# Moving a query's weights into retired memory and the first query ahead of the token loop

## The chip, the cores and the metric

The kernel runs on one core of a Trainium2 chip. The metric is the device time of one execution in microseconds (us). The times shown are the median of three runs. A profile records one execution more; its span, from the first to the last instruction, is a little shorter than the time of the execution it was taken from. Engines are named as in the profile: PE is TensorE (its weight loads, PEld, overlap its products), DVE is VectorE, ACT is ScalarE, POOL is GpSimd, SP is SyncE, whose queue issues nearly all plain transfers here.

## The reference

One graph block over 1250 nodes of 768 features, with 41,250 edges: a graph attention network of two layers and a linear attention side by side, and then a mixture of experts.

```python
xn = layernorm(x)
# graph: 4 heads of 192, then 2 heads of 96, softmax over each node's incoming edges
out2 = gat(gat(norm(xn), W1, 4 heads), W2, 2 heads)
gnn = concat([xn, out2]) @ Wu + bu
# linear attention, 12 heads of 64, phi(t) = elu(t) + 1
q, k, v = phi(xn @ Wq + bq), phi(xn @ Wk + bk), xn @ Wv + bv
kv, ksum = sum_n k[n] v[n]^T, sum_n k[n]            # by head
mix = ((q @ kv) / (q . ksum)) @ Wo + bo
x = x + gnn + mix
# experts: 8, the best two of a gate for each node, hidden width 384
y = layernorm(x)
x = x + sum_e gate_e(y) * (gelu(y @ W1[e] + b1[e]) @ W2[e] + b2[e])
```

## The kernel before, in words

All of it is one function, `gps_block`. Nodes are worked on in NT = 10 tiles of PT = 125, features in KC = 6 slices of 128, and a product of one tile with a 768 x 768 weight is 2 halves of 384 columns with 6 slices each, thus 12 products. They are in float32, and each is two records in the profile.

The stages follow each other in the source: edges are turned into a dense count matrix `AT` and node features are normalised and turned into `xnT` (L358 to L369); first-layer features of all nodes go to `gw`, a view of the tile `kept` (L426 to L436); the first graph attention runs over 4 heads (L542 to L558), the second over 2 (L564 to L574), whose result `o2T` is also a view of `kept`. Then come keys and values (L598 to L629): for each node tile 12 products with `Wk_sb`, 12 with `Wv_sb` and 6 that add k v^T to `kvacc`. L637 to L647 add the values' bias, mask the blocks of the heads, and turn `kvacc` into `kvT` and `ksum` by TensorE transposes (L644, L645) and ScalarE copies (L646, L647). L679 to L684 multiply `kvT` into `Wo_sb`, so that one product with the query gives the linear attention's output. L671 to L677 fold the biases bo and b2 into `bu_b`.

Then the loop over ten node tiles (L767 to L854): `query(t)` (L741 to L764) is 12 products with `Wq_sb` (L750), a chain of steps on VectorE with one exponential on ScalarE (L752 to L761), and six transposes into `qT` (`turn`, L319, L321). `query(t + 1)` is called ahead of tile t's output: 12 products on `xnT` with `Wu_sb` and 12 on `qT` with `Wo_sb` (L780), 4 on `o2T` with `Wu2_sb` (L791), additions on VectorE (L782, L785, L793), a layer norm, the gate and the ranking of the experts. The first query stands ahead of the loop (L766). Last come the experts, with weights in a ring of four buffers of the pool `wt` (L653 to L662, L690, L858, L948 to L957).

What sets the order: a framework that builds the program orders the instructions of each engine itself. Each engine then works through its own list, and instructions wait on semaphores. So a step can stand earlier in an engine's list than in the source: keys' and values' products run in TensorE's gaps of the two attentions, from 132.9 us on. It also places pools in on-chip memory, as stacks from the left and from the right side, and a tile whose place overlaps an earlier one waits until that was last used. Before the change the pool `wt` with Wo, Wq, Wu and Wu2 (L584 to L593) lies where the graph's tiles (`AT`, `mask`, `h2`) were, which are given back at L581 when the second attention is over. The small row tiles bq, bu, bo and bv lie in `kept`, and their loads stand in SP's queue ahead of the weights'.

Of the kernel before, what the change touches and what calls it, by code (L numbers as in the profile page):

```python
# [27 lines left out]
F32 = mybir.dt.float32  # L28
# [5 lines left out]
AF = mybir.ActivationFunctionType  # L34
ALU = mybir.AluOpType
AX = mybir.AxisListType
PSUM = bass.MemoryType.PSUM

N, D = 1250, 768
PT, NT = 125, 10  # L40
KC = D // 128
H1, C1, H2, C2 = 4, 192, 2, 96
HEADS, DH = 12, 64
# [17 lines left out]
def row_bcast(ap, parts):  # L61

    n = 1
    for s in ap.shape:
        n *= s
    return bass.AP(tensor=ap.tensor, offset=ap.offset, ap=[[0, parts], [1, n]])
# [3 lines left out]
def gps_block(ctx: ExitStack, tc: tile.TileContext, x, src, dst, norm_g, norm_b, W1, a_src1, a_dst1,  # L70
# [11 lines left out]
    const = ctx.enter_context(tc.tile_pool(name="const", bufs=1))  # L82
    small = ctx.enter_context(tc.tile_pool(name="small", bufs=3))
    dram = ctx.enter_context(tc.tile_pool(name="dram", bufs=1, space=bass.MemoryType.DRAM))
    big = ctx.enter_context(tc.tile_pool(name="big", bufs=1))
    xr = x.rearrange("(t p) d -> p t d", p=PT)

    def token_rows(t):
# [7 lines left out]

    o0 = H2 * N
    o2T = kept[:C2 + 1, :o0].rearrange("p (h n) -> p h n", h=H2)
    kvT = kept[:, o0:o0 + D].rearrange("p (c f) -> p c f", c=KC)
    ksum, bq_b, bu_b, bo_b = (kept[:PT, o0 + k * D:o0 + (k + 1) * D] for k in range(1, 5))  # L100
    setup = ExitStack()
    fl = setup.enter_context(tc.tile_pool(name="fl", bufs=1, side="right"))
    blocks128 = [(r0, min(T, r0 + 128)) for r0 in range(0, T, 128)]
# [24 lines left out]
    def bank(pool=None, name="mm"):  # L128
        return (pool or mm_p).tile([128, 512], F32, name=name)
# [196 lines left out]
    with tc.tile_pool(name="ma_p", bufs=2, space=PSUM) as ma_p:  # L326
# [111 lines left out]
        with tc.tile_pool(name="hot", bufs=2) as hot, \  # L438
                tc.tile_pool(name="ec_p", bufs=2, space=PSUM) as ec_p:
            for t in range(NT):  # L440
                for i in range(t * NC // NT, (t + 1) * NC // NT):
                    chunk(i, hot, ec_p)
                features(t)
                if t == 1:
                    weights()
                    setup.close()
                    kp = kps.enter_context(tc.tile_pool(name="kp", bufs=1, side="right"))
                    Wk_sb = kp.tile([128, KC, D], F32)
                    Wv_sb = kp.tile([128, KC, D], F32)
                    bk_b = kp.tile([PT, D], F32)  # L450
                    kvacc = kp.tile([128, KC, 129], F32)
                if t == 4:
                    nc.sync.dma_start(Wk_sb, Wk.rearrange("(c p) f -> p c f", p=128))
                    nc.sync.dma_start(Wv_sb, Wv.rearrange("(c p) f -> p c f", p=128))
                    nc.sync.dma_start(bk_b, row_bcast(bk, PT))
# [84 lines left out]
    with tc.tile_pool(name="wp", bufs=3) as wp, tc.tile_pool(name="rb", bufs=1) as rb:  # L540
        with tc.tile_pool(name="ag_p1", bufs=1, space=PSUM) as ag_p:
            for hd in range(H1):  # L542
                ag = ag_p.tile([PT, NT // 2, 512], F32, name="ag")

                def gather1(st, w):
                    for t in range(NT):
                        o = (t % 2) * CG
                        nc.tensor.matmul(ag[:, t // 2, o:o + CG], w[:, t * PT:(t + 1) * PT],  # L548
                                         gw[:, st, hd], start=st == 0 and t % 2 == 0,
                                         stop=st == NT - 1, skip_group_check=True)  # L550

                attend(s1[:, :, hd, 0], s1[:, :, hd, 1], lo1[:, :, hd], wp, rb, gather1)
                v = ag[:, :, :2 * CG].rearrange("p a (b c) -> p a b c", b=2)
                rd = small.tile([PT, NT // 2, 2, 1], F32, name="rd")
                nc.vector.reciprocal(rd, v[:, :, :, C2:C2 + 1])
                for t in range(NT):
                    nc.vector.scalar_tensor_tensor(h2[:, t], v[:, t // 2, t % 2], rd[:, t // 2, t % 2],
                                                   h2[:, t], op0=ALU.mult, op1=ALU.add)  # L558
        ones2 = h2[:, :, :2 * (C2 + 1)].rearrange("p t (h c) -> p t h c", h=H2)[:, :, :, C2:]
        nc.vector.memset(ones2, 1.0)  # L560
        at = 2 * (C2 + 1)
# [19 lines left out]
    graph.close()  # L581


    wt = ctx.enter_context(tc.tile_pool(name="wt", bufs=1))  # L584

    def weight(w):
        t = wt.tile([128, KC, D], F32, name="w", bufs=4)
        nc.sync.dma_start(t, w.rearrange("(c p) f -> p c f", p=128))
        return t

    Wo_sb, Wq_sb, Wu_sb = weight(Wo), weight(Wq), weight(Wu[:D])
    Wu2_sb = wt.tile([96, H2, D], F32)
    nc.sync.dma_start(Wu2_sb, Wu[D:].rearrange("(c p) f -> p c f", p=96))  # L593
    for t, a in ((bq_b, bq), (bu_b, bu), (bo_b, bo)):
        nc.sync.dma_start(t, row_bcast(a, PT))


    for t in range(NT):  # L598
        ky = kp.tile([PT, D], F32, name="ky", bufs=2)
        va = kp.tile([PT, KC, 129], F32, name="va")  # L600
        nc.gpsimd.memset(va[:, :, 128:], 1.0)
        for k in range(2):
# [25 lines left out]
            else:  # L628
                nc.vector.tensor_copy(acc, got)  # L629

    pair = kp.tile([128, 128], F32)
    nc.gpsimd.memset(pair, 0.0)
    nc.gpsimd.memset(pair[0:DH, 0:DH], 1.0)
    nc.gpsimd.memset(pair[DH:128, DH:128], 1.0)
    bv_b = kept[:, o0 + 5 * D:o0 + 6 * D]
    nc.sync.dma_start(bv_b, row_bcast(bv, 128))
    for c in range(KC):  # L637
        acc = kvacc[:, c, :128]
        kcol = kvacc[:, c, 128:]
        nc.vector.scalar_tensor_tensor(acc, bv_b[:, c * 128:(c + 1) * 128], kcol, acc, op0=ALU.mult,  # L640
                                       op1=ALU.add)
        nc.vector.tensor_mul(acc, acc, pair)
        ps = bank()
        nc.tensor.transpose(ps[:, :128], acc, ident)  # L644
        nc.tensor.transpose(ps[:PT, 128:256], kcol.to_broadcast([128, PT]), ident)  # L645
        nc.scalar.copy(kvT[:, c], ps[:, :128])  # L646
        nc.scalar.copy(ksum[:, c * 128:(c + 1) * 128], ps[:PT, 128:256])  # L647
    kps.close()


    fp = ctx.enter_context(tc.tile_pool(name="fp", bufs=1, side="right"))
# [15 lines left out]
    nc.sync.dma_start(Wg_sb, Wg.rearrange("(c p) e -> p c e", p=128))  # L667
    bg_b = fp.tile([PT, NE], F32)
    nc.sync.dma_start(bg_b, row_bcast(bg, PT))
    nc.gpsimd.tensor_add(bu_b, bu_b, bo_b)  # L670
    for k in range(2):  # L671
        half = slice(k * 384, (k + 1) * 384)
        ps = bank()
        for h in range(H2):
            nc.tensor.matmul(ps[:PT, :384], col96[:, 8 + h:9 + h].to_broadcast([96, PT]),
                             Wu2_sb[:, h, half], start=h == 0, stop=h == H2 - 1)
        nc.vector.tensor_add(bu_b[:, half], bu_b[:, half], ps[:PT, :384])  # L677

    for c in range(KC):  # L679
        for k in range(2):  # L680
# [6 lines left out]
    nc.gpsimd.memset(zero, 0.0)  # L687
    nc.sync.dma_start(xl_d[N:], zero)
    nc.sync.dma_start(out[N:], zero[:, :D])
    ring = [expert(fW1[0], fW2[0], fb2[0])]  # L690
    outr = out[:N].rearrange("(t p) d -> p t d", p=PT)
    xlr = xl_d[:N].rearrange("(t p) d -> p t d", p=PT)
    idx = fp.tile([128, NV + 1], I32)
# [4 lines left out]
    with ExitStack() as rs:  # L698
# [7 lines left out]
        def numbers(shape, pattern, base, mult, name, dt=F32):  # L706
# [2 lines left out]
                           allow_small_or_imprecise_dtypes=True)  # L709
            return t  # L710

        before = numbers([PT, NE, NE], [[1, NE], [-1, NE]], 0, 0, "before")
        nc.vector.tensor_scalar(before, before, 0.0, None, op0=ALU.is_gt)
        upto = numbers([128, NE, NE], [[1, NE], [-1, NE]], 0, 0, "upto")
# [23 lines left out]
        cum = rp.tile([PT, NT + 1, NE], F16)  # L738
        nc.vector.memset(cum[:, 0], 0.0)
        inv = g_p.tile([128, NV], F32, name="inv", bufs=1)  # L740
        def query(t):  # L741
            tk = slice(t * PT, (t + 1) * PT)

            qy = qp.tile([PT, D], F32, name="qy")
            qe = qp.tile([PT, D], F32, name="qe", bufs=1)
            for k in range(2):
                half = slice(k * 384, (k + 1) * 384)
                ps = bank()
                for c in range(KC):
                    nc.tensor.matmul(ps[:PT, :384], xnT[:, c, tk], Wq_sb[:, c, half], start=c == 0,  # L750
                                     stop=c == KC - 1)
                nc.vector.tensor_add(qy[:, half], ps[:PT, :384], bq_b[:, half])  # L752
            nc.vector.tensor_scalar(qe, qy, 0.0, None, op0=ALU.min)
            nc.scalar.activation(qe, qe, AF.Exp)
            nc.vector.scalar_tensor_tensor(qy, qy, 0.0, qe, op0=ALU.max, op1=ALU.add)
            nc.vector.tensor_mul(qe, qy, ksum)
            den = rl.tile([PT, HEADS, 1], F32, name="den")
            nc.vector.tensor_reduce(den, qe.rearrange("p (h d) -> p h d", h=HEADS), AX.X, ALU.add)
            nc.vector.reciprocal(den, den)
            q_h = qy.rearrange("p (h d) -> p h d", h=HEADS)  # L760
            nc.vector.tensor_mul(q_h, q_h, den.to_broadcast([PT, HEADS, DH]))  # L761
            qT = qp.tile([128, KC, PT], F32, name="qT")
            turn(qT, qy, mm_p, "mm", nc.scalar.copy)
            return qT  # L764

        qT_next = query(0)  # L766
        for t in range(NT):  # L767
            tk = slice(t * PT, (t + 1) * PT)
            xt = qp.tile([PT, D], F32, name="xt")
# [85 lines left out]
        free = rp.tile([128, NV], F32)  # L855
        nc.vector.tensor_scalar(free, inv, 0.0, nobody, op0=ALU.is_equal, op1=ALU.mult)
        nc.vector.scalar_tensor_tensor(idx[:, :NV], inv, -1.0, free, op0=ALU.add, op1=ALU.add)
        for e in range(1, 4):  # L858
            ring.append(expert(fW1[e], fW2[e], fb2[e]))


# [30 lines left out]


    mix.close()
    sp = ctx.enter_context(tc.tile_pool(name="sp", bufs=2))
    x_p = ctx.enter_context(tc.tile_pool(name="x_p", bufs=1, space=PSUM))
    h_p = ctx.enter_context(tc.tile_pool(name="h_p", bufs=2, space=PSUM))
# [117 lines left out]
```

## Time and profile before

| what | us |
|---|---|
| median of 3 runs | 1166.87 (1166.84 to 1167.5) |
| the profiled execution | 1167.08 |
| its span | 1165.0 |
| edges, features, first-layer weights, to | 196 |
| first graph attention, to | 460 |
| second graph attention, to | 591 |
| rest of keys and values, to | 607.85 |
| first work with Wu, Wu2 and Wo, to | 617.47 |
| loop over node tiles, to | 909 |
| routing and first gather, to | 937 |
| experts, to | 1165 |

The limits of the stages are read from the timeline; the first ones overlap a little. Over the span PE is busy 1066.3 us (92%), DVE 665.0 (57%), ACT 358.1 (31%), POOL 76.5 (7%); the mean granted TensorE clock is 0.975 of full speed. A row of the page gives the busy time of a group of instructions, the mean of one in ns, and the idle time of its engine just before them with what ended it.

### The profile page before, as it was taken

What the parts mean: (1) busy time and instruction counts of PE and PEld (TensorE: products, weight loads), DVE (VectorE), ACT (ScalarE), POOL (GpSimd) and SP (SyncE); (2) the same over time, 40 slices, a digit from 0 to 9 for tenths busy, and PEclk for the clock granted to TensorE, in tenths of its full rate; (3) what the DMA queues carried; (4) which work ended last, traced back from release to release, by engine and by line L of the source; (5) the groups of instructions that cost most, each with busy time, mean ns of one, the idle gap of its engine ahead of it and who ended that gap; (6) DMA issues with size and microseconds to landing.
All of it is one profiled execution on the core that took longest, in us unless ns stands there. A gap on an engine that the chain in (4) does not pass through costs nothing.

```text
span 1165.0 us, 12068 instructions
## 1 busy us (share of the span) xinstructions
PE 1066.3 (92%) x4542; PEld 712.8 (61%) x4542; DVE 665.0 (57%) x1359; ACT 358.1 (31%) x527; POOL 76.5 (7%) x99
## 2 busy tenths in 40 slices
PE   2699998999999989988989999999999599999994
PEld 2596655578787869544545666666666356666652
DVE  7866676669696967688842455555555422222211
ACT  2141114373737364283822211111111011211111
POOL 1000000000000000000000000000000122322321
PEclk9999999999999999989999999999999789999997
DMA  5014000000000001000064011111113637777633
GB/s 158 27 49 168 14 27 1 1 1 1 1 1 1 1 1 54 1 0 1 1 262 165 27 41 41 40 40 41 43 44 117 227 84 189 212 209 217 123 55 56
DMA packets 34823, 79.76 MB, mean 68 GB/s; under 512 B 6799, under 2 KB 14561, under 8 KB 34749
## 3 DMA queue, kind: packets, MB, share of 16 engines
q1 hardware_dynamic: 29148, 59.06, 15.4%
q0 software_dynamic: 5600, 19.77, 8.4%
q8 instruction: 39, 0.64, 0.2%
q14 instruction: 36, 0.29, 0.1%
HBM read 60.48 MB, written 18.34 MB: 68 GB/s over the span
## 4 chain that ended last, share of the span: by engine, by line
PE 70%; DVE 20%; DMA 3%; issue 2%; ACT 2%; POOL 0%; DVEq 0%; SPq 0%; POOLq 0%; ACTq 0%
PE po L780 14%; PE ph L925 9%; PE py L937 7%; PE mm L430 7%; PE mm L607 7%; PE mm L750 7%; DVE scr L515 6%; DVE w L535 5%; DVE w L536 5%; PE ag L548 3%; PE ag L569 2%; PE u L791 2%; PE mm L405 2%; PE px L909 2%; DMA w<-in_L_gnn_Wu_dram 2%
## 5 line engine op out<-in xcount | busy, mean ns | idle before, releaser
L548 PE MATMUL ag<-kept,w 125*125 125x198 f32 x800 | 137.4, 333 | 5.1 <-DVE w L536 4.9
L548 PEld LDWEIGHTS ag<-kept,w 125*125 125x125 f32 x800 | 133.5, 188 | 9.0 <-DVE w L536 9.0
L925 PE MATMUL ph<-xsT,w 128*128 128x384 f32 (+1 forms) x324 | 100.3, 469 | 1.7 <-DVE xsT L912 1.7
L937 PE MATMUL py<-w,hT 128*128 128x384 f32 x300 | 100.6, 486 | 0.0
L430 PE MATMUL mm<-Wg,xnT 128*125 128x400 f32 x240 | 90.2, 513 | 1.1 <-DVE xnT L321 0.6
L607 PE MATMUL mm<-Wv_sb,xnT 128*125 128x384 f32 x240 | 85.7, 489 | 4.8 <-DVE kvacc L627 4.8
L535 DVE TENSOR_TENSOR w<-v,w 125x1250 f32<-125x1250 f32 x60 | 86.4, 1455 | 6.6 <-ACT w L533 5.9
L515 DVE CUSTOM_DVE_ANT_0 scr<-ss_row,mask 125x1250 bf16<-125x1250 f32 x60 | 87.3, 1455 | 0.5 <-ACT ss_row L506 0.2
L780 PE MATMUL po<-w,xnT 128*125 128x384 f32 x240 | 84.5, 501 | 2.9 <-DMA w<-in_L_gnn_Wu_dram 2.9
L536 DVE SCALAR_TENSOR_TENSOR w<-w,AT 125x1250 f32<-125x1250 f32 x60 | 86.5, 1456 | 0.4
L925 PEld LDWEIGHTS ph<-xsT,w 128*128 128x128 f32 x324 | 59.6, 193 | 41.1 <-DVE xsT L912 2.4
L534 ACT ACTIVATE v<-dn_row,sl 125x1250 f32<-125x1250 f32 x60 | 79.3, 1333 | 16.9 <-DVE w L535 16.4
L607 PE MATMUL mm<-Wk_sb,xnT 128*125 128x384 f32 x240 | 84.4, 486 | 0.0
L750 PE MATMUL mm<-w,xnT 128*125 128x384 f32 x240 | 84.2, 489 | 0.0
L780 PE MATMUL po<-w,qT 128*125 128x384 f32 x240 | 80.8, 487 | 0.0
L937 PEld LDWEIGHTS py<-w,hT 128*128 128x128 f32 x300 | 55.3, 190 | 33.9
L912 DVE COPY xsT<-px 128x384 f32<-128x384 f32 x50 | 25.5, 552 | 85.6 <-PE px L909 46.4
L940 DVE TENSOR_TENSOR ys<-py,wb 128x768 f32<-128x768 f32 x25 | 24.0, 958 | 71.3 <-PE py L937 46.2
L780 PEld LDWEIGHTS po<-w,xnT 128*125 128x125 f32 x240 | 43.3, 190 | 31.2 <-DMA w<-in_L_gnn_Wu_dram 3.1
L780 PEld LDWEIGHTS po<-w,qT 128*125 128x125 f32 x240 | 44.1, 188 | 29.5 <-issue 0.2
L607 PEld LDWEIGHTS mm<-Wv_sb,xnT 128*125 128x125 f32 x240 | 42.4, 187 | 31.1 <-DVE kvacc L627 7.0
L750 PEld LDWEIGHTS mm<-w,xnT 128*125 128x125 f32 x240 | 43.6, 188 | 27.6 <-ACT qT L321 0.2
(269 smaller groups left out, 1388.7 us busy)
## 6 DMA issues: line engine op xcount, KB each, us to landing
w<-in_L_ffn_W_dram SPq DMA_DIRECT2D x18, 1152.0 KB
xt<-in_x_dram SPq DMA_DIRECT2D x20, 336.0 KB
wb<-in_L_ffn_b_dram SPq DMA_DIRECT2D x9, 384.0 KB
out_dram<-xt SPq DMA_DIRECT2D x10, 336.0 KB
xl_d<-xl SPq DMA_DIRECT2D x10, 336.0 KB
W_sb<-in_L_gnn_W_dram SPq DMA_DIRECT2D x1, 2304.0 KB
Wk_sb<-in_L_mix_Wk_dram SPq DMA_DIRECT2D x1, 2304.0 KB
Wv_sb<-in_L_mix_Wv_dram SPq DMA_DIRECT2D x1, 2304.0 KB
```

The costliest lines, as they stand in the source:

```text
L430: nc.tensor.matmul(ps[:PT, :2 * (CG + 2)], xnT[:, c, t * PT:(t + 1) * PT], Wg1[:, c, 2 * k:2 * k + 2].rearrange("p h c -> p (h c)"), start ...
L515: nc.vector.tensor_tensor_reduce(scr, ss_row, mask[:, t], 1.0, 0.0, ALU.mult, ALU.max, top[:, t:t + 1])
L534: nc.scalar.activation(v, dn_row, AF.Exp, bias=sl[:, st:st + 1])
L535: nc.vector.tensor_tensor(w, v, w, op=ALU.max)
L536: nc.vector.scalar_tensor_tensor(w, w, 2.0, AT[:, st, :N], op0=ALU.min, op1=ALU.mult)
L548: nc.tensor.matmul(ag[:, t // 2, o:o + CG], w[:, t * PT:(t + 1) * PT], gw[:, st, hd], start=st == 0 and t % 2 == 0, stop=st == NT - 1, ski ...
L607: nc.tensor.matmul(ps[:PT, :384], xnT[:, c, t * PT:(t + 1) * PT], w[:, c, half], start=c == 0, stop=c == KC - 1)
L750: nc.tensor.matmul(ps[:PT, :384], xnT[:, c, tk], Wq_sb[:, c, half], start=c == 0, stop=c == KC - 1)
L780: nc.tensor.matmul(po[k][:, :384], l, r[:, k * 384:(k + 1) * 384], start=i == 0, stop=i == len(parts) - 1)
L912: nc.vector.tensor_copy(xT[:, 3 * a:3 * a + 3, j * 128:(j + 1) * 128], px[:, a, :384].rearrange("p (b n) -> p b n", b=3))
L925: nc.tensor.matmul(ph[:, :n * 128], w[0][:, o:o + 128], xT[:, c, :n * 128], start=c == 0, stop=c == KC - 1)
L937: nc.tensor.matmul(py[:, k, :384], hT[:, f, j * 128:(j + 1) * 128], w[:, o:o + 384], start=f == 0, stop=f == FC - 1)
```

## The change

Four things move, and the computation stays the same. Wq gets a place in `kept`, where the first layer's gathered features are no longer needed after its last head, and its load stands right behind that layer. The pool `kp` of keys and values now closes before a new pool `mp` (ksum, bq, bu and the queries' tiles) and the pool `wt` (Wo, Wu, Wu2, and the experts' ring) open, all three on the right side. `query` is defined ahead of the product of kvT and Wo, and query 0 is called there. The output's bias is folded on VectorE inside the loop's scope, with bo in an `xt` buffer; bv takes a `ky` buffer. The ring starts with two experts instead of one, and the pool `big` with `xnT` is given back before the experts.

```diff
-    big = ctx.enter_context(tc.tile_pool(name="big", bufs=1))
+    first_half = ctx.enter_context(ExitStack())
+    big = first_half.enter_context(tc.tile_pool(name="big", bufs=1))
...
-    kvT = kept[:, o0:o0 + D].rearrange("p (c f) -> p c f", c=KC)
-    ksum, bq_b, bu_b, bo_b = (kept[:PT, o0 + k * D:o0 + (k + 1) * D] for k in range(1, 5))
+    Wq_sb = kept[:, o0:o0 + KC * D].rearrange("p (c f) -> p c f", c=KC)
+    kvT = kept[:, o0 + KC * D:o0 + KC * D + D].rearrange("p (c f) -> p c f", c=KC)
...
+                    kv = ctx.enter_context(tc.tile_pool(name="kv", bufs=1, side="right"))
+                    kvacc = kv.tile([128, KC, 129], F32)
+                    pair = kv.tile([128, 128], F32)
...
+        nc.sync.dma_start(Wq_sb, Wq.rearrange("(c p) f -> p c f", p=128))
         ones2 = h2[:, :, :2 * (C2 + 1)].rearrange("p t (h c) -> p t h c", h=H2)[:, :, :, C2:]
...
-    wt = ctx.enter_context(tc.tile_pool(name="wt", bufs=1))
...
-    Wo_sb, Wq_sb, Wu_sb = weight(Wo), weight(Wq), weight(Wu[:D])
-    Wu2_sb = wt.tile([96, H2, D], F32)
-    nc.sync.dma_start(Wu2_sb, Wu[D:].rearrange("(c p) f -> p c f", p=96))
-    for t, a in ((bq_b, bq), (bu_b, bu), (bo_b, bo)):
-        nc.sync.dma_start(t, row_bcast(a, PT))
...
-    bv_b = kept[:, o0 + 5 * D:o0 + 6 * D]
+    bv_b = kp.tile([128, D], F32, name="ky", bufs=2)
     nc.sync.dma_start(bv_b, row_bcast(bv, 128))
...
+    kps.close()
+
+    mp = ctx.enter_context(tc.tile_pool(name="mp", bufs=1, side="right"))
+    ksum = mp.tile([PT, D], F32)
+    bq_b = mp.tile([PT, D], F32)
+    bu_b = mp.tile([PT, D], F32)
+    wt = ctx.enter_context(tc.tile_pool(name="wt", bufs=1, side="right"))
...
+    nc.sync.dma_start(bq_b, row_bcast(bq, PT))
+    Wo_sb, Wu_sb = weight(Wo), weight(Wu[:D])
+    Wu2_sb = wt.tile([96, H2, D], F32)
+    nc.sync.dma_start(Wu2_sb, Wu[D:].rearrange("(c p) f -> p c f", p=96))
+    for c in range(KC):
         ps = bank()
-        nc.tensor.transpose(ps[:, :128], acc, ident)
+        nc.tensor.transpose(ps[:, :128], kvacc[:, c, :128], ident)
...
-    nc.gpsimd.tensor_add(bu_b, bu_b, bo_b)
-    for k in range(2):
...
+    def query(t):
...
+        qT = mp.tile([128, KC, PT], F32, name="qT", bufs=2)
+        turn(qT, qy, mm_p, "mm", nc.scalar.copy)
+        return qT
+
+    qT_next = query(0)
 
     for c in range(KC):
         for k in range(2):
...
-    ring = [expert(fW1[0], fW2[0], fb2[0])]
+    ring = [expert(fW1[e], fW2[e], fb2[e]) for e in range(2)]
...
+        bo_b = qp.tile([PT, D], F32, name="xt")
+        for t, a in ((bu_b, bu), (bo_b, bo)):
+            nc.sync.dma_start(t, row_bcast(a, PT))
+        nc.vector.tensor_add(bu_b, bu_b, bo_b)
+        for k in range(2):
+            half = slice(k * 384, (k + 1) * 384)
+            ps = bank(u_p, "u")
+            for h in range(H2):
+                nc.tensor.matmul(ps[:PT, :384], col96[:, 8 + h:9 + h].to_broadcast([96, PT]),
+                                 Wu2_sb[:, h, half], start=h == 0, stop=h == H2 - 1)
+            nc.vector.tensor_add(bu_b[:, half], bu_b[:, half], ps[:PT, :384])
...
-        for e in range(1, 4):
+        for e in range(2, 4):
             ring.append(expert(fW1[e], fW2[e], fb2[e]))
...
     mix.close()
+    first_half.close()
```

## The prediction

> **What bounds the kernel now.** First the chain of waits on the page: TensorE holds 70% of it, so where TensorE stands still the time is lost. Then the same chain between 585 and 662 us, in order of time (start, us, what), because there the moved loads stand:
>
> ```profile
> 591.94 18.81 DMA w<-in_L_gnn_Wu_dram
> 610.75 0.04 issue
> 610.79 2.92 PE po L780 x4
> 613.72 3.92 PE mm L675 x8
> ```
>
> A reader of the chain alone would expect 18.81 us from taking this load off it. The timeline of TensorE (start, us, line, idle before and its releaser) says otherwise: it works off keys and values (L607, L621, L644, L645) until 607.85 and waits only then.
>
> ```profile
> 607.58 0.27 PE L645 MATMUL mm<-ident,kvacc 128*125 128x128 f32 x1
> 610.79 2.92 PE L780 MATMUL po<-w,xnT 128*125 128x384 f32 x4 [2.94 <-DMA w<-in_L_gnn_Wu_dram]
> 613.51 4.12 PE L675 MATMUL mm<-Wu_sb,col 96*125 96x384 f32 x8
> ```
>
> The table by stage (window; length and busy us of PE, PEld, DVE, ACT, POOL; granted clock; DMA share; GB/s) shows what the wait leaves behind:
>
> ```profile
> 607.85:610.79 2.94, 0.00 (x1) 0.00 (x0) 0.53 (x4) 0.43 (x2) 2.74 (x15) 0.77 1.04 386
> 610.79:617.47 6.68, 6.68 (x13) 3.64 (x13) 0.63 (x2) 0.00 (x0) 0.13 (x1) 0.59 1.07 355
> 617.47:660.00 42.53, 42.53 (x137) 23.20 (x136) 14.55 (x21) 10.28 (x22) 0.00 (x0) 1.00 0.19 62
> 718.75:747.50 28.75, 28.75 (x110) 17.56 (x109) 15.23 (x41) 5.39 (x8) 0.00 (x0) 1.00 0.14 41
> ```
>
> The clock is 0.59 for 6.68 us, which costs 0.41 x 6.68 = 2.74. So the weights' wait is worth **2.94 + 2.74 = 5.68 us**. From 617.47 to 909 TensorE has no gap (the loop's window 718.75 to 747.5 is busy for its whole length), so whatever is lost or won before the loop reaches the end undiminished.
>
> **What the change does to the order.** I compared the order in which the two built programs hand instructions to each engine (line numbers here and below are those of before). Up to the end of the second attention TensorE, VectorE and ScalarE have the same order. The title's "beside attention" does not come true: the first query's products stand behind the last transposes of keys and values. After them TensorE has, in order: query 0 (12 products), the transposes of query 0, the 12 products of L683, the bias products of L675, query 1, the 12 products of L780 on xnT, the transposes of query 1, the 12 on qT. Before, L780, L675, L683, L750 and half of L780 stood between the wait and the first transposes. Each of these products is two records in the profile, so 12 are 24 records.
>
> **What goes.** The wait for the weights. Wq is loaded at about 460, when the last L548 has read `kept`, with 130 us to spare. Wo, Wu and Wu2 start later than before, not earlier. SP's queue is worked off in order; in it fb comes first, which waits for the end of attention (590.9), and bq stands ahead of the three, which lies where keys' and values' tiles were and waits for the last L607 and L621 and for the last L640 (606.40 + 0.35). With 0.4 of delay (below) bq goes out at about 607.2. In the trace traffic begins 1.9 us after the first issue (590.92; 592.8 by a table in steps of 2 us, which shows 415 to 418 GB/s), and the last of three weights ends 0.9 us after 7.08 MB at 415 GB/s would (17.06 us, to 609.9; used at 610.79). So Wo (0.38 + 2.36 MB, 6.6 us) is there at 616.6, Wu at 622.3, Wu2 at 623.7. They are wanted at 624, 645 and 635: hidden, by query 0, its chain, and the product. −5.68.
>
> **What comes.** (1) Tail of keys and values. The three transposes of L735 (0.15 each at 618 to 628) move in here, the first behind L580 (594.57 + 0.28), so L621 starts 0.4 later; and ScalarE's copies L646/L647 come in an order that frees each bank one copy (0.27) later. Query 0 starts at 608.6 instead of 607.85: 0.75, of which 0.45 moved: +0.3. (2) Query 0's 24 records at 0.323 (7.75 from 643.45 to 651.20) only move. (3) **The new wait.** The transposes need the whole chain of query 0, and nothing stands between. In the trace:
>
> ```profile
> 635.80 0.56 DVE L752 TENSOR_TENSOR qy<-mm,kept 125x384 f32<-125x384 f32 x1 [2.45 <-PE mm L750]
> 636.98 0.84 ACT L754 ACTIVATE qe<-qe 125x768 f32<-125x768 f32 x1 [8.31 <-DVE qe L753]
> 641.10 0.96 DVE L761 TENSOR_TENSOR qy<-qy,den 125x768 f32<-125x768 f32 x1
> 642.11 0.63 PEld L319 LDWEIGHTS mm<-ident,qy 125*128 125x128 f32 x6 [0.52 <-DVE qy L761]
> ```
>
> From the last product (635.76) to the first transpose 6.35 us; before, L780 and L791 filled them (5.8 + 0.65). Now TensorE stands from 616.35 to 622.7, and L683 queues behind the transposes: +6.35. (4) Clock after that gap: below, +2.0. (5) Query 1's chain now has two L782 additions (0.95 each) in it, so 6.35 + 1.9 = 8.3 against 12 products of L780 (7.75): +0.6.
>
> **Hidden, and what it would cost.** bu + bo leave GpSimd (1.81 at 458, idle there) for VectorE (0.95), behind the load of bu, the last of eight transfers after bq: 10.8 MB at 415 GB/s, so at about 636; wanted at 641, behind query 1's first half (+1 per us once it comes after 643). bq is used at 612.4 and lands at about 611. GpSimd's constants (608.05 to 610.92) move up to 590.8; four short VectorE steps that need them stand ahead of L580, ready at 593.4 against 594.57: 1.1 us of cover. The loads of fb, Wg, bg, both zero stores, two wb and the first x rows leave SP at 591 to 600, beside keys and values; `pair` and bv (now in a `ky` buffer) are ready long before 596. Expert 1's weights go out with expert 0's instead of at 872.80, in a stretch without a wait either way. Experts 2 and 3 keep their issues (901, 909, 920), and from there all orders are the same: 0.
>
> **The clock, row against rule.** The trace: a wait of 2.94 took the clock to half, and by a table in steps of 2 us it came back at about 616.2, 5.4 us after work resumed. A second place is the first L925 group after the gaps before 937, clock 0.86 in 13.50 us: a loss of 1.9, so some 3.8 us at half clock. The Trainium skill ("TensorE: Matmul & The Clock Gate", Part 1: The HAM clock gate) speaks against this change: about 3.4 us of idling halve the clock and about 3.4 us of sustained work, in a window that runs on its own, bring it back. By that rule a gap of 2.94 might keep the clock and one of 6.35 never does; the trace differs for the first. By the rule's shortest return: transposes 0.7 longer, then 2.0 us of L683 at 1.29 per product against 0.75 (22 records took 8.14, held by ScalarE), 0.85 lost: 1.55. By the row's 5.4: 0.7 + 1.7 = 2.4. I take 2.0, between them; the sum would be 0.45 lower or 0.4 higher.
>
> **Sum.** +0.3 + 6.35 + 2.0 + 0.6 − 5.68 = **+3.6**. The stage before lost another 0.4 that no row names (its records at 0.323 each, the hold by ScalarE and 5.68 together fall short of the time from 607.85 to 659.7 by about that); it may go too: I take **+3.4**. The profiled execution's 1167.08 (span 1165.0) becomes 1170.5; it lies 0.2 above the median, so the median 1166.87 becomes **1170.3**.
>
> **Rivals.** *Late loads*: bu behind both experts' weights. For it: 355 GB/s in the window above; at 300 GB/s 10.8 MB take 36 us and end at 646, three past the limit. Against: 415 in most of the steps. 1173.3. *The clock holds or returns at once*: the gap costs 6.35 alone, 1168.3. For it: the unknown phase; against: both places above. *Not slower*: TensorE starts L683, whose weights lie ready, while the transposes wait. Twelve products of 0.75 fill the gap from 616.6 on, so 6.35 and the clock's 2.0 go: 3.4 − 8.35, 1161.9; it decides if L683 begins before L319. Against: at 607.85 TensorE idled though Wo and Wq, issued ahead of Wu, were wanted by later products. That the query runs under attention (7.75 less work after it) is excluded by the order.
>
> **Chances.** Forecast 0.70 (own range 1168.9 to 1171.7: ends of the clock, 0.4 unnamed, 0.5 for the delay and chain); late loads 0.10; clock holds 0.11; not slower 0.09. 0.2% is 2.33 us, what a measurement can tell from none: the line is 1169.2. Of the forecast 0.60 lies above; so slower 0.70, same 0.21 (the clock's case and the forecast's low end), faster 0.09. Range 1167.2 to 1174.0.
>
> **What would show it.** The new profile should have no wait of TensorE on Wu; a wait of about 6.3 us ahead of query 0's first transposes, released by VectorE's last qy step; the clock near half behind it; query 0's first record at about 608.6; the addition of bu and bo without a wait on its load; query 1's transposes waiting some 0.6 us; and everything from the third node tile on shifted by one amount. I am wrong if the product of kvT and Wo starts ahead of the transposes, if the gap is under 3 us, if the loads of Wo or bu end a wait, or if the loop or the experts change by themselves.

## The result, and the profile after

The changed kernel takes 1174.47 us, median of six executions (1172.66 to 1177.32), against 1167.61 for the kernel before on the same chip (six, 1166.84 to 1168.92): ratio 1.0055, 95% interval 1.0039 to 1.007. It is slower, as forecast, but by 6.9 us instead of 3.4, and just above the range, which ended at 1174.0. Six more executions, run later, gave 1172.53 against 1167.78, ratio 1.0044 (1.0027 to 1.006); thus the loss is 5 to 7 us. The profiled execution has a span of 1171.06 (1172.86 in all), 6.0 more than before's 1165.03.

The timeline of TensorE after the change, from the end of keys and values to the first output tile (start, us, line, idle time before it and its releaser):

```profile
607.55 0.33 PE L651 MATMUL mm<-ident,kvacc 128*128 128x128 f32 x1 [1.31 <-ACT ksum L654]
...
609.48 9.54 PE L685 MATMUL mm<-kept,xnT 128*125 128x384 f32 x24 [0.18 <-ACT ksum L654]
625.36 1.51 PE L320 MATMUL mm<-ident,qy 125*128 125x125 f32 x6 [6.35 <-DVE qy L696]
626.81 10.33 PE L707 MATMUL mm<-w,kept 128*128 128x384 f32 x24
636.98 2.75 PE L744 MATMUL u<-Wu_sb,col 96*125 96x384 f32 x8
639.56 7.91 PE L685 MATMUL mm<-kept,xnT 128*125 128x384 f32 x24
647.30 7.90 PE L789 MATMUL po<-w,xnT 128*125 128x384 f32 x24
655.30 0.86 PE L320 MATMUL mm<-ident,qy 125*128 125x125 f32 x6
```

Lines are those of the changed kernel: L685 is the query's product (L750 before), L320 the turn (L319), L707 the product of kvT and Wo (L683), L744 the bias (L675), L789 the output (L780), L651 and L652 the transposes of keys and values (L644, L645). The wait on Wu is gone. The wait of 6.35 us on query 0's chain is there, at its place in the order and to the hundredth. Two things were not forecast: a wait of 1.31 among the transposes of keys and values, and query 0's 24 records, which take 9.54 us where query 1's take 7.91.

The same by windows (length and busy us of PE, PEld, DVE, ACT, POOL; granted clock; DMA share; GB/s):

```profile
609.48:619.02 9.54, 9.54 (x24) 5.21 (x24) 0.56 (x1) 0.29 (x2) 0.00 (x0) 0.84 0.94 342
619.01:625.36 6.35, 0.01 (x1) 0.00 (x0) 5.17 (x7) 0.84 (x1) 0.00 (x0) 0.80 1.03 338
625.36:636.98 11.62, 11.62 (x31) 5.70 (x31) 0.00 (x0) 6.22 (x13) 0.00 (x0) 0.81 1.05 359
```

The clock is below 1 in all three stretches, by two spells and not by one. By windows of 1 us it is 0.50 from 609.2 to 612.6, then full, and 0.50 again from 622.8 to 629.7.

What makes the 1.31 us wait is seen in the timeline of all engines:

```profile
606.72 0.35 DVE L628 SCALAR_TENSOR_TENSOR kvacc<-ky,kvacc 128x128 f32<-128x128 f32 x1
607.10 0.29 DVE L630 TENSOR_TENSOR kvacc<-kvacc,pair 128x128 f32<-128x128 f32 x1
607.21 0.26 SPq L645 DMA_DIRECT2D bq_b<-in_L_mix_bq_dram  x1
607.24 0.44 ACT L654 COPY ksum<-mm 125x128 f32<-125x128 f32 x2 [0.69 <-DVE kvacc L628]
```

ksum's first copy needs only a transpose that ended at about 605.4. It goes out at 607.24 because the last L628, the last reader of bv, ended at 607.07. The load of bq leaves SP at the same moment. That the wait is on bv's last reader is shown below, where bv gets another place: the wait goes, and bq's load leaves 1.0 us behind the last products of k and v instead of 3.0.

Where the profiled difference of 6.0 lies, by starts of the same TensorE work in both traces: 0.32 up to the last products of k and v (603.90, 604.22), 4.94 from there to the loop's last products with Wu2 (305.12 us, 310.06), 0.94 from there to the first product of an expert's second layer, L937 before and L947 after (42.07, 43.01), −0.2 in the rest. The third is all clock: the orders are the same, and the mean granted clock of the stretch is 0.72 before and 0.68 after.

```profile
909.02:951.09 42.07, 26.55 (x95) 16.56 (x93) 15.41 (x65) 4.04 (x7) 5.92 (x6) 0.72 0.43 132
```

```profile
914.28:957.29 43.01, 27.77 (x94) 17.45 (x93) 15.38 (x65) 4.14 (x7) 5.96 (x6) 0.68 0.42 129
```

The first is before, the second after. PE's busy time differs by 1.22, in the same work at a lower clock.

### The profile page after: what moved, and what is told of

Read it like the earlier page. It is cut to its first block, busy times and chain, and to the rows that moved or that the text cites. A ratio compares the mean times of both kernels' runs of the same rounds, so it can differ in the third digit from the quotient of the medians.

```text
span 1171.1 us, 12055 instructions
## 1 busy us (share of the span) xinstructions
PE 1067.9 (91%) x4542; PEld 714.6 (61%) x4542; DVE 665.5 (57%) x1360; ACT 358.9 (31%) x527; POOL 74.7 (6%) x98
## 4 chain that ended last, share of the span: by engine, by line
PE 70%; DVE 21%; DMA 2%; issue 2%; ACT 2%; POOL 0%; DVEq 0%; SPq 0%; POOLq 0%; ACTq 0%
PE po L789 13%; PE ph L935 8%; PE mm L600 8%; PE py L947 7%; PE mm L431 7%; PE mm L685 7%; DVE scr L521 6%; DVE w L541 5%; DVE w L542 5%; PE ag L554 3%; PE ag L576 2%; PE u L800 2%; PE mm L406 2%; PE px L919 2%; DMA out_dram<-ys,idx 1%
## 5 line engine op out<-in xcount | busy, mean ns | idle before, releaser
L947 PE MATMUL py<-w,hT 128*128 128x384 f32 x300 | 100.6, 486 | 0.0
L685 PE MATMUL mm<-kept,xnT 128*125 128x384 f32 x240 | 85.3, 496 | 0.2 <-ACT ksum L654 0.2
L789 PE MATMUL po<-w,xnT 128*125 128x384 f32 x240 | 82.5, 494 | 0.0
L789 PE MATMUL po<-w,qT 128*125 128x384 f32 x240 | 80.7, 487 | 0.0
L947 PEld LDWEIGHTS py<-w,hT 128*128 128x128 f32 x300 | 55.3, 190 | 33.9
L685 PEld LDWEIGHTS mm<-kept,xnT 128*125 128x125 f32 x240 | 44.5, 191 | 28.9 <-issue 1.4
L789 PEld LDWEIGHTS po<-w,qT 128*125 128x125 f32 x240 | 44.1, 188 | 29.5 <-issue 0.2
L789 PEld LDWEIGHTS po<-w,xnT 128*125 128x125 f32 x240 | 43.0, 188 | 28.3 <-issue 1.8
```

The source lines that it names most:

```text
L789: nc.tensor.matmul(po[k][:, :384], l, r[:, k * 384:(k + 1) * 384], start=i == 0, stop=i == len(parts) - 1)
L947: nc.tensor.matmul(py[:, k, :384], hT[:, f, j * 128:(j + 1) * 128], w[:, o:o + 384], start=f == 0, stop=f == FC - 1)
```

## The experiments

Single executions of one kernel differ by 4 to 10 us, and a profile is one execution: the last products of k and v start anywhere between 599.71 and 608.05 in these traces, by how often the clock fell in the stages up to 590, whose orders all these kernels share. So beside the medians a stage is compared: from the start of the last products of k and v to the loop's last products with Wu2, and from there to the first product with an expert's second weight. The two traces of the changed kernel agree in both to 0.06. Each row's ratio is to the kernel before, run on the same chip beside it.

| kernel | median, us | ratio (95% interval) | k and v's end to loop's end | from there to first second-layer product |
|---|---|---|---|---|
| before | 1167.61 | | 305.12 | 42.07 |
| after | 1174.47 | 1.0055 (1.0039, 1.007) | 310.06 | 43.01 |
| after, again | 1172.53 | 1.0044 (1.0027, 1.006) | 310.12 | 43.01 |
| turn behind product | 1164.63 | 0.9978 (0.997, 0.9986) | 301.91 | 41.79 |
| bv in kvT's place | 1170.77 | 1.0031 (1.0022, 1.004) | 308.29 | 41.93 |
| both of these | 1162.68 | 0.9964 (0.9949, 0.9978) | 299.86 | 43.01 |
| both, and second query first | 1163.91 | 0.9965 (0.9954, 0.9976) | 299.30 | 43.10 |
| gap filled | 1170.08 | 1.0019 (1.0005, 1.0034) | 308.01 | 42.04 |
| query back | 1174.67 | 1.0067 (1.0051, 1.0082) | 312.04 | 42.94 |
| k/v gap with transposes | 1173.78 | 1.005 (1.0033, 1.0067) | 309.23 | 43.34 |
| k/v gap with products | 1174.44 | 1.0055 (1.0039, 1.0072) | 309.28 | 43.38 |
| Wq only | 1163.43 | 0.9962 (0.9947, 0.9977) | 299.29 | 43.29 |
| Wq only, again | 1162.93 | 0.9959 (0.9948, 0.9969) | 299.28 | 43.03 |
| Wq only, two copiers | 1161.96 | 0.9953 (0.9935, 0.997) | 298.53 | 43.28 |

**The changed kernel again.**

> The changed kernel once more, for more executions. The granted clock of single executions ranges from 0.958 to 0.975 with the time, so a median of six can be off by about 1: 1173 to 1175.5. If the surplus over the forecast were chance, the median would come down to 1171; if it is in the stages, it stays.

The stages stay to the hundredths; the surplus is not chance. The median, 1172.53, fell below the expected 1173: it and the first together leave 5 to 7 us.

**Query 0's turn behind the product.** `query` returns `qy`, and a new `turned` makes `qT`:

```diff
+    q_first = query(0)
-    qT_next = query(0)
     for c in range(KC):
...
             nc.scalar.copy(Wo_sb[:, c, half], ps[:, :384])
+    qT_next = turned(q_first)
```

> After, with query 0's six transposes moved behind the twelve products of kvT and Wo. Gap theory: TensorE goes from query 0's products straight to these, and qy is ready when the transposes come; the wait of 6.35 us and the half clock behind it (1.94) go: 1174.5 - 8.3 = 1166.2. Query 0's own 24 records stay at half clock for a part (9.5 us). Rival, late loads: Wo is not there at 619 and a wait for it takes the place of the old one: about 1174. Rival, the clock behind the gap costs nothing of its own: 1174.5 - 6.35 = 1168.1.

The timeline of TensorE (L710 is the product here):

```profile
611.70 9.62 PE L685 MATMUL mm<-kept,xnT 128*125 128x384 f32 x24 [0.18 <-ACT ksum L654]
621.48 2.36 PE L710 MATMUL mm<-w,kept 128*128 128x384 f32 x6 [0.16 <-DMA w<-in_L_mix_Wo_dram]
624.05 6.84 PE L710 MATMUL mm<-w,kept 128*128 128x384 f32 x18 [0.20 <-ACT w L711]
630.72 0.48 PE L320 MATMUL mm<-ident,qy 125*128 125x125 f32 x3
```

The gap and the half clock behind it are gone; the stage is 8.15 shorter than after's, expected 8.3. Query 0 still runs at half clock for a part, 9.62. Wo is there only 0.16 after query 0's end: the loads are not as early as I had them, and only query 0's slow products hide the last of it. With this one edit the change is faster than the kernel before.

**bv in kvT's place.** kvT's chunk is written only after the same chunk of bv was read, so the two can share a place.

```diff
-    bv_b = kp.tile([128, D], F32, name="ky", bufs=2)
+    bv_b = kept[:, o0 + KC * D:o0 + KC * D + D]
```

> After, with bv loaded into kvT's place instead of a ky buffer. Placement theory: ksum's first copy waits for the last step that reads bv, because bv is a tile of the pool that ksum's pool follows; with bv elsewhere the wait of 1.31 us ahead of L651 goes, query 0 starts at about 608.2 instead of 609.48, and bq and the weights go out 2 us sooner. If the clock was halved at 609.4 because TensorE worked only some 1.7 of the 3.4 us before it, it now holds (about 2.5 of 3.4), query 0's 24 records take 7.8 instead of 9.54, and the sum is -2.9: 1171.6. If the clock falls there all the same: -1.2, 1173.3. Rival, the wait is a copy's queue on ScalarE and not the placement: no change, 1174.5.

```profile
606.00 0.94 PE L614 MATMUL mm<-va,ky 125*128 125x129 f32 x6 [0.41 <-ACT va L610]
...
609.85 8.01 PE L685 MATMUL mm<-kept,xnT 128*125 128x384 f32 x24
624.20 1.51 PE L320 MATMUL mm<-ident,qy 125*128 125x125 f32 x6 [6.35 <-DVE qy L696]
...
654.66 0.86 PE L320 MATMUL mm<-ident,qy 125*128 125x125 f32 x6 [1.44 <-DVE qy L696]
```

The wait of 1.31 is gone: from the last L614 to query 0 it is 3.85 us, against 5.26 in after. Query 0's records take 8.01, so the clock held. Of the 2.9 only 1.8 arrives at the loop's end, for TensorE now waits 1.44 for query 1's chain. VectorE's timeline shows why:

```profile
644.69 0.96 DVE L739 TENSOR_TENSOR bu_b<-bu_b,xt 125x768 f32<-125x768 f32 x1 [1.83 <-DMA bu_b<-in_L_gnn_bu_dram]
```

The addition of bu and bo waits 1.83 for bu's load, and query 1's second half stands behind it. In after the same load ended 0.30 of a wait, hidden (the addition at 644.50).

**Both edits.**

> After, with both edits. Theory: the two add up: 1174.5 - 8.3 - 2.9 = 1163.3; 1165.0 if the clock still falls at query 0. It would then beat the kernel before, by 2 to 4. Rival, late loads: with query 0 done at 616 the product of kvT and Wo waits for Wo (expected at about 614.6), and the gain stops short of the sum.

```profile
611.89 8.01 PE L685 MATMUL mm<-kept,xnT 128*125 128x384 f32 x24
621.04 2.37 PE L710 MATMUL mm<-w,kept 128*128 128x384 f32 x6 [1.14 <-DMA w<-in_L_mix_Wo_dram]
```

1162.68, as expected; the stage is 10.2 below after's instead of 11.2. The 1.0 that is missing is about the wait on Wo, 1.14, that the rival named.

**Query 1 ahead of the product too.** `q_second = query(1)` stands behind `q_first`, and the loop's first pass turns it instead of calling `query(1)`.

> After, with the turn moved, bv in kvT's place, and query 1's products right behind query 0's, ahead of the product of kvT and Wo. Theory: query 1's 7.75 us cover both query 0's chain (6.35) and the rest of Wo's load, so the 1.14 + 0.20 that the product still waited go, and nothing waits on a chain: 1162.7 - 1.3 = 1161.4. Rival, bu: its load lands at about 644, and what queues behind the addition stands: 1163 or more. Rival, the loop gets the same work in another order and the gain is given back at its end: 1162.7.

```profile
608.75 15.75 PE L685 MATMUL mm<-kept,xnT 128*125 128x384 f32 x48
624.33 0.49 PE L320 MATMUL mm<-ident,qy 125*128 125x125 f32 x3
625.13 0.91 PE L794 MATMUL po<-w,xnT 128*125 128x384 f32 x2 [0.31 <-DMA w<-in_L_gnn_Wu_dram]
```

Nothing waits on a chain now, but small waits on Wu (0.31) and Wu2 (0.43) took the place of that on Wo. The stage gains 0.56 of the 1.3, and by the medians nothing can be told.

**The gap filled.** Nine products of query 0's operands, with no reader, behind its own:

```diff
+        if t == 0:
+            ps = bank()
+            for i in range(9):
+                nc.tensor.matmul(ps[:PT, :384], xnT[:, i % KC, tk], Wq_sb[:, i % KC, :384],
+                                 start=i == 0, stop=i == 8)
```

> After, with nine products of query 0's operands (18 records, 5.8 us, their result unused) between query 0's products and its transposes. The wait on VectorE's chain is as long as before, but TensorE works through most of it. If the clock behind the gap is a cost of its own, it goes: the transposes take 0.86 instead of 1.51 and the 24 records of kvT and Wo 8.9 instead of 10.3, in sum -1.9: 1172.5. Rival, the clock behind it is set by something else than TensorE's idling: no change, 1174.5. What of 6.35 is left as a wait is 0.5.

```profile
611.12 9.53 PE L685 MATMUL mm<-kept,xnT 128*125 128x384 f32 x24 [0.18 <-ACT ksum L654]
620.49 5.97 PE L691 MATMUL mm<-kept,xnT 128*125 128x384 f32 x18
627.00 0.86 PE L320 MATMUL mm<-ident,qy 125*128 125x125 f32 x6 [0.54 <-DVE qy L701]
628.10 8.96 PE L712 MATMUL mm<-w,kept 128*128 128x384 f32 x24 [0.24 <-ACT qT L322]
```

The chain is as long as before, but TensorE works meanwhile: transposes 0.86 instead of 1.51, product 8.96 instead of 10.33, the stage −2.05, the median 2.45 below that of the changed kernel run beside it. So the half clock behind the gap is a cost of its own, of 2.0.

**Query 0 back ahead of the loop, late loads kept.** The call moves to its old place, nothing else.

> After, with query 0 called ahead of the loop again, all loads as in after. Theory, the loads are late and only query 0 hides them: TensorE stands from 609.3 until Wo is there (12.0 us behind bq's issue by the runs with the turn moved, thus about 619.2), a wait of some 9.9 and the half clock behind it of 2, against 6.35 + 1.94 + 1.65 in after: +4 over it, 1178. Rival, the early query alone makes the loss and the late loads are harmless: about 1164, as in the kernel with the turn moved.

```profile
614.97 11.37 PE L706 MATMUL mm<-w,kept 128*128 128x384 f32 x24 [9.71 <-DMA w<-in_L_mix_Wo_dram]
```

TensorE stands 9.71 us for Wo, and the product behind it takes 11.37 instead of 8.96. In the stage that is 2.0 more than after, expected 4. The expectation's own terms (9.9 and 2 against 6.35, 1.94 and 1.65) make 2.0, so the 4 was a slip in the sum. The rival's 1164 is out. So without the early query the late loads cost more than query 0's chain does with it.

**What halves the clock over query 0.** The 1.31 us wait is filled with nine transposes in one kernel, with two products in another (their results unused):

```diff
+        if c == 1:
+            pf = fill_p.tile([128, 512], F32, name="pf")
+            for i in range(9):
+                nc.tensor.transpose(pf[:, :128], kvacc[:, 3 + i % 2, :128], ident)
```

> After, with nine more transposes (result unused) in the wait of 1.31 us that ksum's placement makes among the transposes of keys and values, some 1.0 us of work there. It asks what halves the clock over query 0. If TensorE's share of work in the window counts (1.8 of 3.41 us in after, about 2.8 here), the clock holds and query 0's 24 records take 8.0 instead of 9.54: about -1.6 in the stage. If transposes don't count as work, it falls all the same: 9.5, no change beyond 0.4.

> The same place filled with two products of 384 columns (four records, 1.3 us, result unused) instead of transposes. Both theories expect the clock to hold here, share of work (about 3.0 of 3.41) and kind of work: query 0's 24 records at 8.0. If it falls here too, neither the share nor the kind in that window sets it, and the cause of query 0's half clock is open.

TensorE of the first (L692 is the query, L658 the filling):

```profile
606.82 1.29 PE L658 MATMUL pf<-ident,kvacc 128*128 128x128 f32 x9 [0.41 <-DVE kvacc L630]
...
609.81 8.01 PE L692 MATMUL mm<-kept,xnT 128*125 128x384 f32 x24
...
625.62 10.99 PE L714 MATMUL mm<-w,kept 128*128 128x384 f32 x24
```

In both kernels query 0's records take 8.01, though query 0 starts as late behind k and v as in after (5.43 and 5.70, against 5.26). So work in the wait holds the clock, and transposes do for it as well as products. The filling shortens the pause and adds to the work at once; which of the two counts, these kernels do not separate (the last section has a longer pause, behind which the clock held). But the stage gains only 0.8 of the 1.6: the product behind the gap takes 10.99 and 10.88 instead of 10.33, because the clock came back later there: 4.5 and 4.3 us behind the product's start, against 2.9 in after. By the medians nothing is gained.

**Wq alone.** Wq goes to `kept` as in after; Wo, Wu and Wu2 keep the place and time of before (from 590.9 on), and query 0 its place ahead of the loop. ksum, bq and bu are in a pool on the left side. The rest of the change stays (the bias on VectorE, bv in a `ky` buffer, two experts at the start of the ring), so this is the change without its late loads and its early query, not before with one edit.

```diff
+    mps = ExitStack()
+    mp = mps.enter_context(tc.tile_pool(name="mp", bufs=1))
-    mp = ctx.enter_context(tc.tile_pool(name="mp", bufs=1, side="right"))
...
-    qT_next = query(0)
...
+        qT_next = query(0)
         for t in range(NT):
```

> One part alone: Wq in kept behind the first layer as in after; Wo, Wu and Wu2 where and when before loads them (left side, 590.9), query 0 in the loop's scope as before, the small tiles and the bias of the output as in after but on the left side. With 2.36 MB less ahead of them the three weights are there by about 605, so nothing waits at 607.85. If the wait on Wu was worth its 2.94 and the half clock behind it 2.74: 1167.6 - 5.7 = 1161.9. Rival, the clock falls at 609.4 whatever the weights do, since the end of keys and values leaves TensorE half idle: -2.94 alone, 1164.7. Rival, traffic of the load beside work costs as much as it saves: 1167.

> The kernel with Wq alone moved, once more. From keys' and values' last products to the first transposes of the loop it took 57.16 us against 63.55 before, thus 6.4 less, and its median 4.0 less than before's with executions from 1156 to 1166. Theory, the stage decides and the rest is the clock's windows elsewhere: the stage takes 57.2 again and the median lies 4 to 6.4 below before's. Rival, something later gives the gain back: the stage takes 57.2 and the loop or the experts take over 1 us more than before's 241.6 and 256.0.

```profile
610.32 8.96 PE L683 MATMUL mm<-w,kept 128*128 128x384 f32 x24
619.12 2.75 PE L720 MATMUL u<-Wu_sb,col 96*125 96x384 f32 x8
```

And the window of these two, with the clock at 1.00:

```profile
610.32:621.87 11.55, 11.55 (x34) 5.16 (x33) 0.55 (x3) 6.17 (x14) 2.13 (x15) 1.00 0.93 313
```

There is no wait and no half clock between keys' and values' transposes and the loop. The stage is 5.83 shorter than before's in both traces, for 5.68 forecast as the worth of the wait. The medians lie 4.0 and 4.8 below before's: 1.0 to 1.2 is given back in the stretch behind the loop (43.29 and 43.03 against 42.07), which is the clock again, as the last section shows; so the rival holds for about a fifth of the gain.

**Two copiers.** In that kernel every second copy of the product goes to VectorE: `(nc.vector.tensor_copy if k else nc.scalar.copy)`.

> Wq alone moved, and every second copy of the product of kvT and Wo on VectorE instead of ScalarE. Theory: the product's 24 records took 8.96 because each waits for ScalarE's copy of the bank before; with two engines they take 7.75 to 8.0: 1.0 less than the kernel with Wq alone. Rival: VectorE's copies queue behind a step that waits for GpSimd's constants until about 613, and the product stands there: no gain, or up to 1 more.

The stage gains 0.75, and the order changed with it: bias and output products now stand between the 24 records, so their own time can't be read. 1161.96 is the lowest median of all, but its interval overlaps that of Wq alone.

## Why the prediction was half right

The direction, the wait that goes and the two large costs of the early turn (6.35 and 2.0) came true. The step that failed is the worth put on the wait on Wu: 2.74 of the −5.68 was half clock that I took to go with that wait, and a wait of 1.31 among the transposes of keys and values, which the prediction does not have, kept 1.63 of it and cost 0.88 more than the 0.3 that I had for that stretch. A second term, the experts, was put at 0 because their order stays, and the clock behind the loop took 0.94.

- **The wait on Wu goes, the loads are hidden: right, with wrong sizes.** Wo was wanted at 626.8 and there by about 619, by an estimate from the kernels that wait for it. I had Wo at 616.6, which is 9.1 behind its issue (607.52); it took 11.7 to 12.0 in the three kernels that wait for it (issued 609.75, 609.36 and 603.01, used at 621.48, 621.04 and 614.97). bu, put at 636, came at about 644.5, past the 643 that I had set as its limit. Each estimate had let a transfer have the full 415 GB/s in the order of issue; windows of 1 us show 204 to 409 between 611 and 628. bu's load ended a wait of 0.3 on VectorE, hidden from TensorE, and only because query 1 was later too (its first half was added at 643.63): in the kernel with bv moved it cost TensorE 1.44. That it stayed hidden is luck more than forecast.
- **−5.68: half right, the step that failed.** 2.94 went. The 2.74 of half clock I had put down to the wait on Wu as if the clock held without it. It does hold where no other wait stands there (Wq alone, 1.00 up to the loop). In after it fell at the same place, 609.2 (609.5 before), with no wait on Wu, and query 0's records took 9.54 instead of 7.91: 1.63 of it stayed.
- **+0.3 for the end of keys and values: 1.18, part of the same failure.** Query 0 started at 609.48 (+1.63, 0.45 of it moved work), not at 608.6. I had read the order of ScalarE's copies but taken each to wait for its own bank; ksum's place makes the first wait for bv's last reader. The two are one cause: without that wait the clock holds too (8.01 in three kernels with bv moved or the wait filled as single edits).
- **+6.35: right. +2.0 of clock behind it: right,** 0.65 in the transposes and 1.37 in the product, 2.02; the filled gap takes 2.05 away.
- **+0.6 for query 1's chain: 0.** From query 1's last product to its transposes it was 7.83, not 8.3, and L789's 7.90 covered it.
- **Experts: 0 forecast, about +0.8,** by 0.94 behind the loop and −0.2 at the end. The orders are the same, the clock is not.

With these, 3.4 + 0.88 + 1.63 − 0.6 = 5.3 up to the loop's end, measured 0.32 + 4.94 = 5.26; with 0.8 behind it, 6.0, the difference of the spans. The 3.4 has in it 0.2 taken off for a loss that no row names; no run shows where it went, so the sum closes that well partly by luck. None of the rivals took place: the clock did not hold, the product did not start ahead of the transposes, and late loads ended no wait of TensorE in after itself.

## What to carry to other kernels

A load moved early is worth what its wait costs only if the others stay where they were: Wq in the free place, with Wo, Wu and Wu2 left in theirs, took 4 to 5 us off; letting these three wait for the end of keys and values turned this into a loss, with the early query (1.0044 and 1.0055 of before) and without it (1.0067). When a step with a chain on another engine is moved ahead, move only its products and leave the step that needs the chain's end behind the next independent work; here six transposes moved by twelve products made 8 us. A tile in a pool that follows another can wait for that pool's last reader, long after its own input is ready: look for the late reader (here bv's) and give its data another place.

## What the hardware showed unexpectedly

The clock changes on a grid of 3.41 us. In after its spells at half are 3.4 and 6.9 us long (609.2 to 612.6, 622.8 to 629.7) and start 13.6 apart, thus one, two and four steps. Some half a step's work, scattered, was not enough to hold it. PE's busy time in the window ahead of query 0, in after, with bv moved, and with transposes in the wait:

```profile
605.77:609.18 3.41, 1.76 (x10) 1.21 (x10) 1.58 (x6) 1.67 (x9) 0.00 (x0) 1.00 0.28 41
```

```profile
607.60:611.01 3.41, 2.92 (x14) 1.95 (x15) 1.54 (x6) 2.08 (x12) 0.00 (x0) 1.00 0.64 150
```

```profile
606.25:609.66 3.41, 2.84 (x21) 2.21 (x19) 1.27 (x6) 1.88 (x10) 0.00 (x0) 1.00 0.29 50
```

Behind the first the clock fell to half, behind the others it held. In all traces, in the windows around the end of keys and values, it fell behind 1.31 to 1.82 us of work (before, after twice, turn moved, gap filled, query back) and held behind 2.41 to 2.93; nothing between was seen there. In after no single pause in that window is longer than 1.31. The Trainium skill ("TensorE: Matmul & The Clock Gate", Part 1: The HAM clock gate), which I had weighed as a rule on idling for a whole window, speaks of a free-running window of activity; the size of the window agrees, and here scattered short waits were enough.

The busy time of the records is not exactly what the clock follows. In the kernel with products in the wait, a window at the end of query 0 had 1.73 us of work and then a pause of 1.69. The clock held behind it, though with the turn moved it fell behind as much work, 1.73, most of it transposes:

```profile
616.92:620.33 3.41, 1.73 (x6) 0.69 (x4) 1.12 (x2) 0.78 (x2) 0.00 (x0) 1.00 1.03 405
620.33:623.74 3.41, 0.00 (x0) 0.00 (x0) 3.05 (x4) 0.23 (x1) 0.00 (x0) 1.00 1.04 390
```

In before, a window that its records fill (76.98 to 80.39, where 16 of 28 are products with 2 columns) was followed by half clock. So the limit at this place is near half a window, it seems to move with the kind of work, and what exactly is counted stays open.

The grid of windows also ties places together that share no work. The stretch behind the loop took 41.79 to 42.07 or 42.94 to 43.38 us in the same order of instructions, by when in its first pauses the clock fell: 7.0 to 7.6 us after the last products with Wu2 in before and in the kernels with the turn moved, bv moved and the gap filled, 5.5 to 6.7 in the others. The spell at half is 23.9 us, seven steps, in each trace of the first group and 27.3, eight steps, in each of the second. So a change can gain or lose 1 us of clock 300 us later. That this is so for every execution was not measured: only one or two traces of each kernel show it.
